# Slot-attention and FFN on one core: the weight products and the read-out of a unit made during the next unit

## The chip, the cores and the metric

One core of a Trainium2 chip runs the whole program. Its engines are TensorE (PE in the profile; its weight loads are PEld), VectorE (DVE), ScalarE (ACT), GpSimd (POOL) and SyncE (SP, which here issues most DMAs). The metric is the time of one execution on the device in microseconds, lower is better. A kernel's time is the median of its runs; beside it stands one profiled execution, whose trace gives the durations used below.

## The reference

Four sequences of 512 tokens (D = 512) go through LayerNorm, a slot attention with 16 heads, a residual, LayerNorm again, and a gated FFN whose weights are rounded to fp8 values (but computed in fp32), and a second residual. For each head, with 64 slots (M), keys of 64 and values of 128:

```python
z = jax.lax.cumlogsumexp(s, axis=2)
g = jnp.exp(jnp.concatenate([z[:, :, :1], z[:, :, :-1]], axis=2) - z)
p = jnp.exp(s - z)
# step over tokens
hk = hk * g_t[:, :, None, :] + k_t[..., None] * p_t[:, :, None, :]
ok = jnp.einsum('bhk,bhkm->bhm', q_t, hk)
pv = softmax(ok)
hv = hv * g_t[..., None] + p_t[..., None] * v_t[:, :, None, :]
ov = jnp.einsum('bhm,bhmv->bhv', pv_t, hv)
# then
o = o * rsqrt(mean(o * o) + EPS) * g_norm_weight
o = o * (gate * sigmoid(gate))
x = x + o.reshape(b, t, VALUE_DIM) @ Wo
x = x + ffn(layernorm(x))
```

## The kernel before

The kernel takes the recurrence apart into blocks of 64 tokens: products within a block under a triangular mask, and sums of states from block to block. A unit is a pair of heads (g, 0 to 7) of one sequence (b, 0 to 3). There are 32 units in the order b = 0, 1 for each g, then b = 2, 3 for each g. `first_unit` makes the first; `attention` makes each of the others, and within it carries out what is left of the unit in front (`before`). The FFN of the four sequences follows. The instructions of every engine stand in the order in which the code issues them, so each engine is a queue.

Precise products of wide matrices (128x512 results) are made of three products of parts rounded to fp32r: projections s, k, q, g (L517), v (L554) and o (L876), 12 matmuls for a projection and 6 for each of the four o blocks. Small products are plain fp32: transposes (L569, four for each tile: e, kn, oT, okn, w), and products of 64 rows: a = q and k within a block (L590), b = slot weights within a block (L590), sk and sv, the key and value states (L611), ok, the slot scores (L717 from states, L723 from a), and ov, the read-out (L803 from states, L813 from b).

The order of a unit before, as TensorE sees it: s, k, q, then the transposes e and kn; in an even unit v in four parts; between these the transposes oT of the unit in front; a, sk, sv; the two halves of g; ok; six matmuls of the front unit's o; okn; ten of o; w; four of o; b; four of o; ov. So b and ov belong to the unit itself. The work on other engines:

- `read_within` (L807) squares ov on ScalarE (L823) and sums it on VectorE (L824, L825), and GpSimd raises the sum to the power -1/2 (L828). `scale_output` (L833, VectorE, first head) and `scale_other` (L839, ScalarE in four pieces, second head) scale ov by it into og. They stand in the next unit, behind its s and k. `turn_output` (transposes oT, L855), `high_output` (L861) and `split_output` (L865, L866) make og times the gate into the three parts that o is made from.
- `softmax` (L738, L740), `softmax_exp` (L745), `slot_weights` (transposes w, then wT on VectorE, L784) and `move_weights` (L777, ScalarE, two copies) make the slot weights.
- `add_up` (L620) adds the states up: a copy (L622), a sum (L623) and, along the blocks, two more sums (L625). GpSimd then shifts states between halves of the partitions (L689 to L691 for keys, L768 to L771 for values).
- `project_output` (L870) copies each finished o block on ScalarE to y (L887), and GpSimd issues its accumulating DMA to the stream in HBM (L888).
- `fill`, `next_step`, `other`, `piece` take single pieces of side work from a list: splitting the next weights (L260, L266, L267; first half), LayerNorm of later sequences (L340 to L374), and rounding the FFN's weights (`quantize`, L451; second half).

PSUM has eight banks: four in a ring (`bank`, for transposes and most small products), two "proj" buffers (`ps3`, for projections and o blocks, taken in turn) and two "acc" buffers (`ps2`: a, ok and ov before; the FFN's sums later):

```python
            if name[0] == "a":
                p = ps2.tile([P, T], F32, tag="acc", name=f"ps_{name}_{h}")
            else:
                if turn[0] in held:
                    turn[0] = (turn[0] + 1) % BANKS
                p = bank(f"ps_{name}_{h}")
```

A buffer can be written again when its last reader is done. The token block that LayerNorm reads is loaded whole (four blocks of 128 tokens in one DMA, `load_tokens`, L308) and kept for the FFN's residual.

## Time and profile before

| what | value |
|---|---|
| median of 3 runs | 1402.9 us (1402.51 to 1403.57) |
| the profiled execution's own time | 1400.63 us |
| its span, first to last instruction | 1398.7 us |
| granted TensorE clock | 1.0 throughout |
| TensorE matmul, weight load busy | 1376.8, 1106.1 us |
| VectorE, ScalarE, GpSimd busy | 906.1, 701.4, 358.3 us |
| first FFN matmul, from the span's start | 1119.72 us |
| an odd unit, an even unit (second half, from s to s) | 28.58, 39.33 us |

A group's line gives start or line, engine, operation, output and inputs with shapes, count and duration; in square brackets stands how long the engine was idle in front of it and which instruction ended that. Matmuls overlap in TensorE's pipeline, so what one costs is read from start to start, not from its duration.

### The profile page before, as it was taken

To read this page: it belongs to the slowest core of one execution; us is meant where nothing else is said; L and a number is where in the kernel's file an instruction comes from. 1 tells how busy PE (TensorE), PEld (TensorE's weight loads), DVE (VectorE), ACT (ScalarE), POOL (GpSimd) and SP (SyncE) were. 2 spreads that over 40 slices of the span, in tenths; PEclk is the share of its full clock that TensorE was granted. 3 is DMA by queue.
4 is the path that set the end of the run, shared out by engine and by line. 5 is a ranking of instruction groups with operands and counts; after the bars stand their busy time and mean duration, and the time that the engine had idled before them with its cause. 6 is when DMAs were issued, how large, how long until landed. Compare 5 with 4: busy or idle time off the path is not lost.

```text
span 1398.7 us, 31065 instructions
## 1 busy us (share of the span) xinstructions
PE 1376.8 (98%) x13163; PEld 1106.1 (79%) x13163; DVE 906.1 (65%) x1625; ACT 701.4 (50%) x1327; POOL 358.3 (26%) x433
## 2 busy tenths in 40 slices
PE   8899999999999999999999999999999999999998
PEld 4678888888888877788888888887888788888886
DVE  6677656765676578756876677767776653535343
ACT  4557556655665566455544555455445633222221
POOL 2233323322333243223322332234124310000000
PEclk9999999999999999999999999999999999999999
DMA  8266646575556655456646574657455641101000
GB/s 323 105 195 228 198 113 174 190 248 148 149 184 216 179 176 154 119 167 197 185 133 189 189 216 110 189 189 232 116 174 172 217 117 16 61 0 60 1 31 30
DMA packets 80889, 213.03 MB, mean 152 GB/s; under 512 B 6168, under 2 KB 35120, under 8 KB 75568
## 3 DMA queue, kind: packets, MB, share of 16 engines
q1 hardware_dynamic: 62224, 177.49, 34.3%
q0 software_dynamic: 18528, 33.58, 15.8%
q8 instruction: 103, 1.69, 0.5%
q14 instruction: 34, 0.28, 0.1%
HBM read 107.23 MB, written 108.00 MB: 154 GB/s over the span
## 4 chain that ended last, share of the span: by engine, by line
PE 91%; DVE 5%; ACT 2%; DMA 1%; issue 1%; POOL 0%; SPq 0%; ACTq 0%; POOLq 0%; DVEq 0%
PE ps_o L876 14%; PE ps_g L517 11%; PE ps_v L554 10%; PE ps_s L517 6%; PE ps_fg L1099 6%; PE ps_fu L1099 6%; PE ps_k L517 6%; PE ps_q L517 5%; PE ps_fd L1160 3%; PE ps_fe L1160 3%; PE ps_ov L803 2%; PE ps_ov L813 2%; PE ps_sv L611 2%; PE ps_oT L569 2%; PE ps_b L590 1%; PE ps_w L569 1%
## 5 line engine op out<-in xcount | busy, mean ns | idle before, releaser
L876 PE MATMUL ps_o<-w_o,oT 128*128 128x512 f32 x768 | 212.0, 410 | 1.9 <-ACT w_o L260 1.2
L517 PE MATMUL ps_g<-xs,w_g 128*128 128x512 f32 x744 | 179.1, 396 | 0.0
L554 PE MATMUL ps_v<-w_v,xs 128*128 128x512 f32 x720 | 171.5, 393 | 0.0
L517 PEld LDWEIGHTS ps_g<-xs,w_g 128*128 128x128 f32 x744 | 137.1, 188 | 33.4 <-issue 5.3
L888 POOL DMA_DIRECT2D stream<-y x128 | 112.6, 940 | 192.7 <-ACT y L887 184.8
L876 PEld LDWEIGHTS ps_o<-w_o,oT 128*128 128x128 f32 x768 | 134.1, 188 | 30.9 <-ACT y L887 2.1
L554 PEld LDWEIGHTS ps_v<-w_v,xs 128*128 128x128 f32 x720 | 132.9, 188 | 26.2
L689 POOL COPY moved<-sk 64x192 f32<-64x192 f32 x32 | 10.9, 340 | 449.9 <-DVE sk L625 449.9
L1120 DVE SCALAR_TENSOR_TENSOR h<-ps_fu,scol,act 128x512 f32<-128x512 f32 x48 | 36.0, 750 | 114.5 <-PE ps_fu L1099 114.5
L1099 PE MATMUL ps_fg<-xs,wf 128*128 128x512 f32 x384 | 95.6, 391 | 0.0
L887 ACT COPY y<-ps_o 128x512 f32<-128x512 f32 x128 | 74.4, 581 | 40.9 <-PE ps_o L876 39.7
L1099 PE MATMUL ps_fu<-xs,wf 128*128 128x512 f32 x384 | 94.8, 389 | 0.0
L517 PE MATMUL ps_s<-xs,w_s 128*128 128x512 f32 x372 | 93.4, 400 | 0.0
L517 PE MATMUL ps_q<-xs,w_q 128*128 128x512 f32 x372 | 90.0, 391 | 2.1 <-DVE eT L642 2.1
L517 PE MATMUL ps_k<-xs,w_k 128*128 128x512 f32 x372 | 89.4, 389 | 0.0
L1099 PEld LDWEIGHTS ps_fu<-xs,wf 128*128 128x128 f32 x384 | 72.1, 188 | 15.0
L1099 PEld LDWEIGHTS ps_fg<-xs,wf 128*128 128x128 f32 x384 | 71.6, 188 | 14.8 <-issue 0.2
L517 PEld LDWEIGHTS ps_q<-xs,w_q 128*128 128x128 f32 x372 | 69.6, 188 | 17.0 <-DVE eT L642 2.5
L517 PEld LDWEIGHTS ps_s<-xs,w_s 128*128 128x128 f32 x372 | 67.4, 188 | 17.9 <-issue 3.4
L561 ACT COPY v<-ps_v 128x512 f32<-128x512 f32 x60 | 35.1, 585 | 92.8 <-PE ps_v L554 92.8
L517 PEld LDWEIGHTS ps_k<-xs,w_k 128*128 128x128 f32 x372 | 69.8, 188 | 14.5
L1126 ACT CAST both<-h 128x512 fp32r<-128x512 f32 x48 | 29.8, 620 | 96.7 <-DVE h L1120 96.7
(167 smaller groups left out, 2795.7 us busy)
## 6 DMA issues: line engine op xcount, KB each, us to landing
stream<-y POOLq DMA_DIRECT2D x128, 256.0 KB, 7.0
split_v<-w_v SPq DMA_DIRECT2D x4, 3072.0 KB, 11.5
split_g<-w_g SPq DMA_DIRECT2D x8, 1536.0 KB, 8.1
split_o<-w_o SPq DMA_DIRECT2D x8, 1536.0 KB, 7.1
w_v<-split_v SPq DMA_DIRECT2D x4, 3072.0 KB, 16.0
w_g<-split_g SPq DMA_DIRECT2D x8, 1536.0 KB, 7.3
w_o<-split_o SPq DMA_DIRECT2D x8, 1536.0 KB, 8.8
rounded<-qw SPq DMA_DIRECT2D x36, 256.0 KB, 2.2
```

What stands on the lines that cost most here:

```text
L517: nc.tensor.matmul(p, wt[self.nm][:, j, at : at + P], xs[self.b][i][:, c, :], start=(i == 0 and c == 0), stop=(i == 2 and c == KC - 1),)
L554: nc.tensor.matmul(p, xs[b][i][:, c, n * P : (n + 1) * P], wt["v"][:, j, c * 2 * HV : (c + 1) * 2 * HV], start=(i == 0 and c == 0), stop=( ...
L561: nc.scalar.copy(to, p)
L569: nc.tensor.transpose(pt[:, n, :], s, by)
L611: nc.tensor.matmul(pts[sub][half(h), n, :], left[half(sub), n, h * M : (h + 1) * M], right[half(sub), n, right0 + h * width : right0 + (h ...
L876: nc.tensor.matmul(self.p, self.oT[:, i, h, n * P : (n + 1) * P], wt["o"][:, j, h * D : (h + 1) * D], start=(i == 0 and h == 0), stop=(i = ...
L887: nc.scalar.copy(y, self.p)
L888: nc.gpsimd.dma_start(stream[self.b][n * P : (n + 1) * P, :], y, accum_op=ALU.add)
L1099: nc.tensor.matmul(pp, w[:, c * P : (c + 1) * P], xs[b][k][:, c, :], start=(c == 0 and k == 0), stop=(c == KC - 1 and k == 1),)
L1120: nc.vector.scalar_tensor_tensor(h, pu, us, act, ALU.mult, ALU.mult)
L1126: nc.scalar.copy(hi, h)
L1160: nc.tensor.matmul(sums[n], parts[k][:, n * P : (n + 1) * P], fw[c][2], start=(c == 0 and k == 0), stop=(c == NFC - 1 and k == 1),)
```

## The change

In every unit from the second on, b, the read-out ov and all that follows it are made for the unit in front, in one stretch with the unit's own a, key states and value states. `scale_output` and `scale_other` stand behind that stretch, with the load of ScalarE's silu table ahead of `scale_other`. The gate's second half follows, then ok, then oT of the unit in front, its parts, and the sums of the value states along the blocks (`add_along`); then the gate's first half, the softmax, and o in runs of 16 and 8. b takes the "acc" buffers and a the ring's banks; ov and ok stay in "acc". The last unit's b and ov are made at the head of the FFN. Tiles that now live longer have tags or second buffers of their own (eT, sg1, moved_v, moved_w, wT, the masked b). In o, the first two matmuls of the second block stand ahead of the last two of the first block. The two halves of a head pair are split side by side (`split_output`). LayerNorm's tokens are loaded in four single blocks into LayerNorm's own two tiles, the third and fourth as tiles come free, and normalised in place; the FFN loads its residual anew (`load_rest`), for the first sequence too. LayerNorm's measuring of the third and fourth block moves behind their loads. The FFN weights are rounded from three buffers instead of four, with four rounds in an even unit, two in the units of g = 1 and one in other odd units.

```diff
-    def load_tokens(b, source, pool=one, tag="tokens"):
-        x1[b] = pool.tile([P, NT, D], F32, tag=tag, name=f"x1_{b}")
-        nc.sync.dma_start(x1[b], source[b].rearrange("(n p) d -> p n d", p=P))
+    blocks_in = {}
+    def load_block(b, n, source):
+        blocks_in[b, n] = two.tile([P, D], F32, tag="xn", name=f"tokens_{b}_{n}")
+        nc.sync.dma_start(blocks_in[b, n], source[b][n * P : (n + 1) * P, :])
+    def load_tokens(b, source):
+        for n in range(2):
+            load_block(b, n, source)
+    def load_rest(b, places):
+        x1[b] = []
+        if len(places) == 1:
+            pool, tag = places[0]
+            x = pool.tile([P, NT, D], F32, tag=tag, name=f"x1_{b}")
+            nc.sync.dma_start(x, stream[b].rearrange("(n p) d -> p n d", p=P))
+            x1[b] = [x[:, n, :] for n in range(NT)]
+            return
+        for n, (pool, tag) in enumerate(places):
+            x = pool.tile([P, D], F32, tag=tag, name=f"x1_{b}_{n}")
+            nc.sync.dma_start(x, stream[b][n * P : (n + 1) * P, :])
+            x1[b].append(x)
...
-            if name[0] == "a":
+            if name[0] == "b":
...
-            a = one.tile([P, NT, SB], F32, tag=f"a{h}", name=f"{name}_{h}")
+            a = one.tile([P, NT, SB], F32, tag=f"{name[0]}{h}", name=f"{name}_{h}")
...
-    def add_up(own, pts, state):
+    def add_pairs(own, pts, state):
         nc.scalar.copy(own, pts[0])
         nc.vector.tensor_tensor(state, pts[1][:, : NT - 1, :], own[:, : NT - 1, :], ALU.add)
+    def add_along(state):
         for n in range(1, NT - 1):
             nc.vector.tensor_tensor(state[:, n, :], state[:, n, :], state[:, n - 1, :], ALU.add)
...
             self.left = [(n, i, j, h) for n in range(NT) for i, j in PAIRS for h in range(HG)]
+            self.left[4:8] = self.left[6:8] + self.left[4:6]
+            self.p = {}
...
-            self.z = one.tile([P, T], F32, tag="th", name=f"z_{self.u}")
+            self.z = one.tile([P, T], F32, tag="ok", name=f"z_{self.u}")
...
         def move_states(self):
             svo = self.svo
-            self.moved_v = moved = one.tile([P, NT, DV], F32, tag="kT", name=f"moved_v_{self.u}")
+            add_along(self.sv)
+            self.moved_v = moved = one.tile([P, NT, DV], F32, tag="moved_v", name=f"moved_v_{self.u}")
...
-            self.wT = one.tile([P, T], F32, tag="kn", name=f"wT_{self.u}")
+            self.wT = one.tile([P, T], F32, tag="wT", name=f"wT_{self.u}")
...
-            self.sg.append(one.tile([P, T], F32, tag=f"sg{h}", name=f"sg_{self.u}_{h}"))
+            self.sg[h] = (one, two)[h].tile([P, T], F32, tag=f"sg{h}", name=f"sg_{self.u}_{h}")
...
-        def split_output(self, h):
-            hi, lo, less = (self.oT[:, i, h, :] for i in range(3))
-            nc.vector.tensor_tensor(lo, self.sg[h], hi.bitcast(F32), ALU.subtract)
-            nc.vector.scalar_tensor_tensor(
-                less, lo.bitcast(F32), -1.0 / DELTA, hi.bitcast(F32), ALU.mult, ALU.add
-            )
+        def split_output(self):
+            parts = [[self.oT[:, i, h, :] for i in range(3)] for h in range(HG)]
+            for h, (hi, lo, _) in enumerate(parts):
+                nc.vector.tensor_tensor(lo, self.sg[h], hi.bitcast(F32), ALU.subtract)
+            for hi, lo, less in parts:
+                nc.vector.scalar_tensor_tensor(
+                    less, lo.bitcast(F32), -1.0 / DELTA, hi.bitcast(F32), ALU.mult, ALU.add
...
+    def silu():
+        nc.scalar.preload_act_table_set("silu_and_others")
...
         X.slots()
         load("s")
-        before.scale_output()
         need("k")
         X.keys()
         load("k")
         if not even:
             turning(True)
-        before.scale_other()
         X.running_sum()
         fill(more)
         need("q")
         X.queries()
         load("q")
-        if not even:
-            turning(True)
         X.turn_e()
+        X.turn_k()
+        X.inverse()
+        X.move_queries()
         if even:
-            X.turn_k()
-            X.inverse()
-            next_step()
             need("v")
-            X.values(0)
-            fill(more)
-            X.values(1)
-            before.turn_output(0)
-            before.high_output(0)
-            before.turn_output(1)
-            before.high_output(1)
-            fill(more)
-            X.values(2)
-            before.split_output(0)
-            next_step()
-            fill(more)
-            X.values(3)
-            before.split_output(1)
-            next_step()
-            fill(more)
-        else:
-            X.inverse()
-            before.turn_output(0)
-            X.turn_k()
-            before.turn_output(1)
-            before.high_output(0)
-            before.high_output(1)
+            for n in range(NT):
+                X.values(n)
+                next_step()
+                fill(more)
+        elif b > 1:
+            fill(1)
         if units[1] == (g, b):
             need(f"xs_{b - 1}")
+        while turned():
+            other(1)
+        before.weight_slot()
         X.query_key()
         X.key_states()
+        before.read_states()
+        before.read_within()
         X.value_states()
-        X.move_queries()
-        if not even:
-            before.split_output(0)
-            before.split_output(1)
-            fill(1)
+        before.scale_output()
+        silu()
+        before.scale_other()
         need("g")
+        X.gate(1)
+        X.gate_silu(1)
+        X.slot_scores()
+        before.turn_output(0)
+        before.high_output(0)
+        before.turn_output(1)
+        before.high_output(1)
+        before.split_output()
+        X.move_states()
         X.gate(0)
         X.gate_silu(0)
-        if even or b > 1:
-            next_step()
-        X.gate(1)
-        X.gate_silu(1)
         exp_and_log()
         load("g")
         if even:
...
         ahead()
         gated()
         need("o")
-        X.slot_scores()
-        before.project_output(6)
-        X.move_states()
         X.softmax()
+        before.project_output(8)
         X.softmax_exp()
-        fill(1)
-        before.project_output(10)
+        before.project_output(8)
         X.slot_weights()
         X.move_weights()
+        fill(1)
         next_step()
-        before.project_output(4)
-        X.weight_slot()
-        before.project_output(4)
+        before.project_output(8)
         load("o")
         X.softmax_sum()
-        if even or b > 1:
-            fill(1)
-        X.read_states()
         fill(1)
-        if even:
-            next_step()
-            if turned():
-                other(1)
-        X.read_within()
-        if not even and b < 2:
-            next_step()
-            if turned():
-                other(1)
+        next_step()
+        fill(1)
         return X
...
+                if (b, c) == (0, 0):
+                    before.weight_slot()
                 h = ffn_hidden(b, c)
                 if b == 0 and c == 0:
+                    before.read_states()
+                    before.read_within()
                     before.scale_output()
+                    before.left.sort()
                     before.scale_other()
                 if b == 0 and 0 < c < 3:
                     before.turn_output(c - 1, 2)
                     before.high_output(c - 1)
-                    before.split_output(c - 1)
+                    if c == 2:
+                        before.split_output()
                 if b == 0 and 2 < c < 3 + NT:
                     before.project_output(6)
+                if c == 1 and b == 0:
+                    load_rest(0, FFN_TOKENS[0])
                 if c == 1 and b + 1 < B:
-                    load_tokens(b + 1, stream, *((two, "v"), (one, "tokens"), (one, "y"))[b])
+                    load_rest(b + 1, FFN_TOKENS[b + 1])
```

## Prediction

> **What bounds the kernel now.** I read the page's busy times and chain first, then the timeline of one unit in the second half (786 to 815 us), all engines, then the waits of TensorE.
>
> ```profile
> PE 1376.8 (98%) x13163; PEld 1106.1 (79%) x13163; DVE 906.1 (65%) x1625; ACT 701.4 (50%) x1327; POOL 358.3 (26%) x433
> PE 91%; DVE 5%; ACT 2%; DMA 1%; issue 1%; POOL 0%; SPq 0%; ACTq 0%; POOLq 0%; DVEq 0%
> ```
>
> TensorE (PE) is busy 98% of the span and is 91% of the chain; its waits add up to some 17 us, with none over 3.0 us. So a part of the change is worth only what it takes from, or puts into, the stream of matmuls. That stream has a price of its own for changing between wide matmuls (128x512) and small ones (64-row products, transposes):
>
> ```profile
> 809.69 0.66 PE L569 MATMUL ps_w<-idents,ok 128*128 128x128 f32 x4
> 810.10 1.18 PE L876 MATMUL ps_o<-w_o,oT 128*128 128x512 f32 x4
> 811.20 0.69 PE L590 MATMUL ps_b<-wT,eT 64*64 64x64 f32 x32
> 811.83 1.20 PE L876 MATMUL ps_o<-w_o,oT 128*128 128x512 f32 x4
> 812.95 0.32 PE L803 MATMUL ps_ov<-moved_v,moved_w 64*64 64x128 f32 x1
> ```
>
> Read start to start. Undisturbed, 12 matmuls of ps_k took 2.72 us (789.12 to 791.84), 0.227 each, so four should take 0.91; here four ps_o between small groups took 1.10 and 1.12, and ps_b took 0.63 where ps_a, with the same shapes but small neighbours, took 0.51.
>
> **The change, by stretches of one odd unit (28.58 us from s to s: 786.27 to 814.85).** All starts below are of that unit, or of the next where ps_w and ps_o are meant.
>
> *Taken out: changes of kind.* b and ov leave the place between ps_o's and join kn, a, sk and sv in one small stretch. From the end of w to the end of s the old order took 1.10 + 0.63 + 1.12 + 1.90 (ov) + 2.85 (s) = 7.60. The same work costs 1.91 (eight ps_o behind w) + 0.515 (b priced as a) + 1.79 (ov without its 0.11 us exit) + 2.72 (s as k) = 6.93. The rest of the unit (oT behind ok, g in two halves, o in 16 + 8) gains another 0.11 by the same counting: 0.78 in all. In an even unit sk and sv no longer interleave (0.18 back): about 0.6. The 31 units behind the first are 16 odd and 15 even: 16 x 0.78 + 15 x 0.62 = **-21.8 us**.
>
> *Added: a wait at ps_ok.* ps_b, ps_ov and ps_ok now share the two "acc" buffers, in this order, within one unit. Until now s, k and q (8.3 us) lay between the read-out ov and ps_ok's group; now it is sv and half of g. ps_ok may not start before ov's results have been read by scale_output (VectorE) and scale_other (ScalarE), and these wait for a chain over three engines:
>
> ```profile
> 786.27 3.01 PE L517 MATMUL ps_s<-xs,w_s 128*128 128x512 f32 x12
> 786.37 1.09 ACT L823 ACTIVATE og<-ps_ov 128x512 f32<-128x512 f32 x2 [0.77 <-PE ps_ov L813]
> 787.00 1.28 DVE L824 TENSOR_REDUCE rs<-og 128x4 f32<-128x512 f32 x2 [2.28 <-ACT og L823]
> 788.32 0.17 DVE L825 SCALAR_TENSOR_TENSOR rs<-rs,sq 128x8 f32<-128x8 f32 x1
> 788.64 1.67 POOL L828 TENSOR_TENSOR rs<-rs,mhalf 128x8 f32<-128x8 f32 x1 [2.42 <-DVE rs L825]
> 790.34 0.69 DVE L833 TENSOR_TENSOR og<-ps_ov,rs 128x512 f32<-128x512 f32 x1 [0.32 <-POOL rs L828]
> 792.58 1.15 ACT L839 ACTIVATE og<-ps_ov,rs 128x128 f32<-128x128 f32 x4
> 797.49 1.13 PE L611 MATMUL ps_sv<-v,e 64*64 64x128 f32 x28
> 798.56 5.76 PE L517 MATMUL ps_g<-xs,w_g 128*128 128x512 f32 x24
> ```
>
> Squares, two sums, rs, GpSimd's power, then the scaling: the power ends at 790.31. L839 came late only because it was queued behind kT; freed of that it runs 790.35 to 791.50. TensorE left ov at 786.27, or 786.17 without the exit. So ps_ok can go 5.38 us after ov (791.50 + 0.05 - 786.17). What lies between now: sv 1.07 (797.49 to 798.56) and half of g (5.68 / 2, plus 0.10 for the change of kind) 2.94: 4.01. TensorE stands 1.37 us in each of 31 units: **+42 us**. The ACT table load that moves ahead of scale_other (1.28 us) and the svo copy (0.59) end 1.1 us before the power does, so they cost nothing; without that cover they would lengthen the wait by what is left of them. Over the 32 units the quickest power ended 0.1 sooner and the slowest 0.3 later than here: 1.25 to 1.65 per unit, 39 to 51 in all.
>
> *Added: a wait at the next unit's ps_s.* With b and ov gone, only eight ps_o (1.91) lie between w and s. ps_s takes the buffer of the third ps_o, whose copy to y stands on ScalarE behind the two copies of moved_w, and these wait for wT:
>
> ```profile
> 810.38 0.69 DVE L784 TENSOR_TENSOR wT<-ps_w,rzT 128x512 f32<-128x512 f32 x1 [0.33 <-PE ps_w L569]
> 811.10 0.82 ACT L777 COPY moved_w<-wT 64x256 f32<-64x256 f32 x2 [1.00 <-DVE wT L784]
> 811.95 0.59 ACT L887 COPY y<-ps_o 128x512 f32<-128x512 f32 x1
> ```
>
> From w's start (809.69) that copy ends at 812.54, 2.85 later; s is wanted 0.41 + 1.91 = 2.32 after w: 0.56 of standing with the 0.03 handoff. In ten units of the first half a weight split (L260, 622 ns) is queued ahead of that copy: 1.18. In four units with LayerNorm transposes around the eight ps_o it is about 0.3. 10 x 1.18 + 17 x 0.56 + 4 x 0.3 = **+22.5 us**. Ends: 12, if the split comes later in the queue and the copy earlier; 30, if every unit pays some 0.97.
>
> *The softmax.* VectorE's queue from ps_ok to w: okT 0.75, two sg 1.40, lo 1.37, less 1.38, two sv sums, mx 0.69, ok 0.69, then ScalarE's exp 0.63. The sv sums (L625) move here from behind ps_sv:
>
> ```profile
> L625 DVE TENSOR_TENSOR sv<-sv x64: 291/705/874, 44.2 to 1105.2; 128x128 f32<-128x128 f32 x64
> ```
>
> 291 with GpSimd at rest (two cases), 705 beside its additions. In the new place GpSimd has nothing to do until they are done: 0.58 for two. With 0.2 ahead of okT and 0.15 of handoffs the chain is 7.85; TensorE's cover is oT 0.8 + g 2.85 + okn 0.36 + sixteen ps_o 3.9 = 7.9. It just fits: **0**. At the row's mean (555 each, 1.11) it would be late by some 0.47 in 31 units, +15: the upper end. The lower end is -4, the 0.12 by which w already waits for exp today.
> The Trainium skill (GPSIMD Engine Reference, Specifications) says that GpSimd shares its SBUF interfaces with VectorE and collides with instructions of two SBUF inputs. By it the sums cost their undisturbed 291, so nothing here; by the mean of the row it would be +15.
>
> *Small terms.* In odd units kn's copy ends just when sk wants it, so sk waits for the handoff: 16 x 0.05 = 0.8. In the eight odd units of the second half the last quantize step (two of 0.69) stands ahead of b's masks on VectorE, which then start 2.25 us after q instead of 1.6; the second is 0.4 late for ov, which needs its buffer: 3.2. In the FFN the first oT has 3.9 us of cover (16 matmuls and a change of kind) for scale_output, which needs 4.9: 1.0. Sum **+5**. Lifted: 0.67 at ps_ok in three even units (706.93 to 746.94 is 40.01 against 39.33), and two stops at oT for a bank held by LayerNorm (1.26 and 1.45): **-4.7**, at worst +3 if the block loads take their place. The token loads by block (four of 256 KB for one of 1 MB, per LayerNorm, and four more for the first FFN block) go through SP's queue; the weight loads behind them are issued a unit ahead (28 us; the slowest, w_v, lands in 16.0), which hides a block's wait for its tile. If that cover went, a late weight would stop a projection for as long as the load is late. GpSimd's powers stand ahead of its moved_v work and behind moved, which ends 0.3 before the power is due: nothing.
>
> Sum: -21.8 + 42 + 22.5 + 0 + 5 - 4.7 = +43. The profiled execution took 1400.6, of which 1398.7 is the span; its sum is 1443.6. The median of the runs lies 2.3 above that execution: **1446 us**.
>
> **Rivals.** *The softmax chain binds as well* (20%): VectorE late at w by 0.47 in every unit, 1446 + 15 = 1461. For it: a margin of 0.05 in 7.9. Against: the two undisturbed sums.
> *The wait at ps_s is mostly hidden* (11%): if something else delays TensorE between w and s, or the copy slips ahead; 1446 - 22 = 1424. Against: ScalarE's queue is in program order.
> *ps_ok does not wait* (7%; the case that ends on the other side). Place: the first matmuls of ps_ok; price: the whole 42 us; it decides if the chain from ov to scale_other takes 4.0 us instead of 5.4. Then -21.8 + 22.5 + 5 - 4.7 = +1, 1404: no change; with half of the wait at ps_s gone too, 1393. Against: in none of the 32 units did the power end sooner than 4.0 us after ov, and scale_other's 1.15 comes behind it.
> *The change doesn't do what it says*: b and ov do stand beside a, sk and sv in the order of the built program, in all 31 units; no chance is kept for it.
>
> **How the numbers follow.** Forecast 62%, 1446, its own range 1432 to 1458. The softmax rival takes the range up to 1466; the ends of ps_s's wait and of the switches take it down to 1424. Below lie the case without the ps_ok wait and half of the tail. A measurement here can tell 0.2% (2.8 us) from no change: faster 4%, same 3%, slower 93%.
>
> **What would show it.** In the new profile: ps_o in runs of 16 and 8 with fewer slow first matmuls; TensorE idle some 1.3 us ahead of ps_ok, released by VectorE's og or ScalarE's og; idle some 0.5 ahead of ps_s, released by ScalarE's y; w waiting no longer than today; sv sums near 291. An odd unit of 29.9 us. The prediction is wrong if TensorE arrives at ps_ok and finds it free, or if w's wait grows past 0.5.

## The result, and the profile after

After the change the kernel takes 1524.4 us (median of four runs, 1517.3 to 1528.1) against 1402.7 before (1400.8 to 1403.6): a ratio of 1.086, 95% interval 1.082 to 1.090. It is slower, as forecast, but by 122 us where 43 were forecast, and outside the range. The profiled execution took 1528.06 us, its span 1526.4.

The page of after first: busy times, granted clock in 40 slices, and the chain by engine.

```profile
PE 1394.3 (91%) x13163; PEld 1130.3 (74%) x13163; DVE 874.7 (57%) x1625; ACT 700.8 (46%) x1327; POOL 336.0 (22%) x433
PEclk9899999999999999799999999999999999999999
PE 67%; DVE 11%; DMA 9%; ACT 6%; POOL 4%; issue 3%; SPq 0%; POOLq 0%; DVEq 0%; ACTq 0%
```

The matmuls are the same 13163. TensorE was busy 98% of the span and 91% of the chain; now it is busy 91% and holds 67% of the chain. Two shares are new in kind: DMA has 9% where it had 1%, "issue" 3% where it had 1%. The prediction's only term for DMA is the +3 that the block loads could cost at worst. The list of TensorE's waits shows where they fall (tile and line that waited, what it waited for; us in total, times, longest):

```profile
PE ps_ok L750 <- DVE og L867: 25.7, 27, 1.2
PE ps_ov L837 <- DVE b L623: 19.1, 6, 5.5
PE ps_s L544 <- ACT y L923: 16.1, 27, 0.9
PE ps_xn L380 <- DVE tokens L371: 14.1, 5, 8.0
PE ps_a L617 <- ACT qT L685: 9.4, 6, 2.8
PE ps_ov L847 <- issue: 5.1, 2, 2.7
PE ps_s L544 <- DMA w_s<-split_s: 5.1, 1, 5.1
...
PE ps_e L596 <- ACT eT L675: 4.6, 3, 2.0
PE ps_q L544 <- DVE eT L674: 4.4, 3, 1.6
PE ps_o L912 <- DVE w_o L267: 4.1, 2, 3.6
```

Two kinds stand here side by side. Rows one and three have 27 entries, all short: they come in nearly every unit, and they are the two waits that the prediction names. The other rows have one to six entries of up to 8.0 us: stops of some units only, which the prediction does not have. No row has ps_w: the softmax rival did not come.

Cut the span at the first matmul of each ps_s and it falls into units (us; steady: what an undisturbed unit of the second half has more than before, 1.15 in an odd unit (29.71 to 29.72 against 28.55 to 28.57) and 1.06 in an even one (40.39 against 39.33)):

| stretch | before | after | more | steady part |
|---|---|---|---|---|
| head, unit 0 | 52.8 | 62.6 | 9.8 | 0 |
| unit 1 | 45.1 | 46.9 | 1.8 | 1 |
| units 2 to 13 | 408.4 | 457.4 | 49.0 | 13 |
| units 14, 15 | 62.6 | 76.9 | 14.2 | 2 |
| unit 16 | 41.6 | 50.6 | 9.0 | 1 |
| units 17 to 30 | 478.0 | 509.2 | 31.3 | 13 |
| unit 31 | 31.3 | 40.4 | 9.2 | 1 |
| FFN | 279.0 | 282.4 | 3.5 | 0 |

So the steady cost, 16 x 1.15 + 15 x 1.06, is about 34 us (some 2 less, since three even units were 0.67 longer before). The forecast was 43. The column "more" sums to 128, the difference of the two profiled spans (the medians differ by 122). The other 94 are in places, and these must be explained one by one. The windows of three units of after (window, us; then busy us and count of PE, PEld, DVE, ACT, POOL; granted clock, DMA share, GB/s) show the two kinds:

```profile
1060.66:1090.37 29.71, 28.25 (x349) 23.33 (x349) 18.63 (x36) 16.78 (x34) 9.70 (x12) 1.00 0.78 253
598.20:643.70 45.50, 33.02 (x358) 26.26 (x357) 26.34 (x52) 20.76 (x42) 12.58 (x17) 0.87 0.32 77
643.70:694.30 50.60, 44.18 (x413) 35.55 (x413) 26.13 (x52) 20.39 (x38) 9.85 (x13) 0.95 0.38 120
```

In the undisturbed odd unit TensorE stands 1.46 us at the full clock. Units 15 and 16 stand 12.5 and 6.4 us, at a granted clock of 0.87 and 0.95: there a stop also makes the matmuls behind it slower. This price can be read by itself; in such stretches the granted clock is 0.50 (after, columns as above):

```profile
642.32:649.14 6.82, 5.43 (x13) 4.30 (x14) 1.39 (x3) 0.00 (x0) 0.70 (x1) 0.50 1.05 352
1007.54:1014.37 6.83, 3.97 (x73) 4.00 (x77) 2.80 (x9) 0.29 (x1) 1.79 (x3) 0.50 0.29 83
```

After has twelve of them, 61.4 us together; before has none from 5 us to 1397 us.

### The profile page after: what moved, and what is told of

Its sections match the earlier page's. It is cut to its first block, busy times and chain, and to the rows that moved or that the text cites. A ratio compares the mean times of both kernels' runs of the same rounds, so it can differ in the third digit from the quotient of the medians.

```text
span 1526.4 us, 31065 instructions
## 1 busy us (share of the span) xinstructions
PE 1394.3 (91%) x13163; PEld 1130.3 (74%) x13163; DVE 874.7 (57%) x1625; ACT 700.8 (46%) x1327; POOL 336.0 (22%) x433
## 4 chain that ended last, share of the span: by engine, by line
PE 67%; DVE 11%; DMA 9%; ACT 6%; POOL 4%; issue 3%; SPq 0%; POOLq 0%; DVEq 0%; ACTq 0%
PE ps_o L912 9%; PE ps_v L581 7%; PE ps_g L544 6%; PE ps_fg L1108 6%; PE ps_fu L1108 6%; PE ps_s L544 4%; PE ps_k L544 4%; POOL rs L862 3%; PE ps_q L544 3%; PE ps_fd L1169 3%; PE ps_fe L1169 3%; PE ps_ov L837 2%; DVE rs L858 2%; PE ps_oT L596 2%; DMA rounded<-qw 2%
## 5 line engine op out<-in xcount | busy, mean ns | idle before, releaser
L912 PE MATMUL ps_o<-w_o,oT 128*128 128x512 f32 x768 | 198.2, 406 | 6.3 <-DVE w_o L267 4.1
L544 PE MATMUL ps_g<-xs,w_g 128*128 128x512 f32 x744 | 189.2, 403 | 2.3 <-issue 2.3
L912 PEld LDWEIGHTS ps_o<-w_o,oT 128*128 128x128 f32 x768 | 139.2, 191 | 39.6 <-ACT y L923 6.1
L544 PE MATMUL ps_s<-xs,w_s 128*128 128x512 f32 x372 | 97.3, 412 | 24.8 <-ACT y L923 16.1
L544 PEld LDWEIGHTS ps_q<-xs,w_q 128*128 128x128 f32 x372 | 69.6, 188 | 19.9 <-issue 5.6
```

Of the source, the lines that this page charges most:

```text
L544: nc.tensor.matmul(p, wt[self.nm][:, j, at : at + P], xs[self.b][i][:, c, :], start=(i == 0 and c == 0), stop=(i == 2 and c == KC - 1),)
L912: nc.tensor.matmul(self.p[n], self.oT[:, i, h, n * P : (n + 1) * P], wt["o"][:, j, h * D : (h + 1) * D], start=(i == 0 and h == 0), stop=( ...
```

## The experiments

All runs beside runs of the kernel before on the same chip. "Against after" is by medians.

| run | median us | ratio to before, 95% | against after |
|---|---|---|---|
| ok_in_ring | 1493.7 | 1.065 [1.061, 1.068] | -30.7 |
| y_before_moved | 1528.1 | 1.090 [1.088, 1.092] | +3.7 |
| spread_splits | 1527.7 | 1.089 [1.085, 1.094] | +3.3 |
| rounding_as_before | 1514.2 | 1.080 [1.079, 1.082] | -10.2 |
| two_more_places | 1508.7 | 1.075 [1.073, 1.077] | -15.7 |
| blocks_in_time | 1511.7 | 1.078 [1.076, 1.080] | -12.7 |
| all_five | 1449.5 | 1.033 [1.032, 1.035] | -74.9 |
| nothing_late | 1432.6 | 1.022 [1.021, 1.023] | -91.8 |
| splits_like_before | 1428.2 | 1.018 [1.016, 1.020] | -96.2 |
| last_blocks | 1417.2 | 1.011 [1.010, 1.013] | -107.2 |
| b_at_head | 1410.8 | 1.007 [1.005, 1.009] | -113.6 |
| pieces_after_w | 1420.2 | 1.012 [1.010, 1.013] | -104.2 |

### The two waits of every unit

**ok_in_ring.** ps_ok takes two banks of the ring, so it no longer needs the buffers that ov holds.

```diff
-            pok = [
-                ps2.tile([P, T], F32, tag="acc", name=f"ps_ok_{self.u}_{sub}") for sub in range(2)
-            ]
+            pok = [bank(f"ps_ok_{self.u}_{sub}") for sub in range(2)]
```

> The changed kernel with ok's two results in banks of the ring instead of the two acc buffers; nothing else. Theory A: ok waits only because it takes the buffers that ov's scaling still reads (25.7 us over 27 units in the trace of the changed kernel). In the ring it need not; the next reader of the scaled og is oT, 1.37 us of ok later, and the chain of 5.38 us behind ov then has 4.01 + 1.37 us of cover, so at most 0.1 us a unit is left: 20 to 26 us less, about 1500. Rival B: the wait only moves, to oT or to the softmax chain: no more than 7 us less, 1517 or above.

Measured: 30.7 us less. The wait is gone from the list, and an undisturbed odd unit is 28.36 long instead of 29.71 to 29.72 (window of this run, columns as above):

```profile
1029.92:1058.28 28.36, 27.95 (x349) 23.07 (x349) 18.62 (x36) 16.74 (x34) 9.69 (x12) 1.00 0.82 267
```

That is more than the 20 to 26 of theory A. So the wait costs 1.36 in an odd unit (1.37 was forecast) and 1.32 to 1.35 in an even one. The row above shows only 0.95 for one (25.7 / 27): the rest is in starts that the wait delays without counting as idle time. Over 31 units 1.36 would be 42; it was 30.7 by the medians and 37.7 by the two profiled spans. What is missing lies in units with other stops: 23 and 26, for instance, have a stop of 2.2 and 2.6 us called "issue" in this run. The mechanism and its price stand; it is not what the prediction missed.

**y_before_moved.** The third o block's copy to y comes ahead of moved_w on ScalarE:

```diff
         X.slot_weights()
-        X.move_weights()
         fill(1)
         next_step()
         before.project_output(8)
+        X.move_weights()
```

> The changed kernel with the two moved_w copies issued behind the last two y copies instead of ahead of them. Theory A: ps_s waits (16.1 us over 27) because the y copy of the third o block queues behind them on ScalarE: 13 to 16 us less, about 1509. Rival B: ps_s waits for the copy's own length and the matmul before it; what is ahead of it in the queue doesn't matter: within 4 us of the changed kernel.

Measured: no gain; the median is 3.7 higher, within the scatter of the two kernels' runs. By its number that is rival B. Its cause is not rival B's, though: where nothing else is late, a window of an odd unit of the second half is 0.72 shorter than after's:

```profile
1057.41:1086.41 29.00, 27.96 (x350) 23.40 (x348) 18.62 (x36) 16.94 (x33) 9.65 (x13) 1.00 0.80 254
```

The trace has the wait's cause as forecast, too: on ScalarE the copies to y stand behind the two of moved_w, which waited 1.44 for wT (last bracket: idle before, and what ended it; this is after's timeline).

```profile
1059.13 0.83 ACT L811 COPY moved_w<-wT 64x256 f32<-64x256 f32 x2 [1.44 <-DVE wT L818]
1059.98 1.08 ACT L923 COPY y<-ps_o 128x512 f32<-128x512 f32 x2
```

In the first half the saved 0.72 went into the next stop: ps_q's wait for eT rose from 4.4 to 19.9 us. A small wait just in front of a larger one is worth nothing alone.

### The first half: where the pieces of the weight splits stand

In the first half each weight is loaded into one of two raw buffers and split by pieces (L260 on ScalarE, then VectorE). Before the change such pieces (placed by `fill`) began on VectorE at 0, 6.4, 17.8, 22.6 and 27.1 us from s in unit 3. In the new order they begin at 1.7, 3.0, 6.9, then 32.9 and 34.8 (the unit is stretched). When three pieces come at once the two raw buffers are empty, and the next load cannot have landed. ScalarE's queue is in order; in unit 3 of after:

```profile
148.22 0.64 ACT L698 ACTIVATE rzT<-rzT 128x512 f32<-128x512 f32 x1
152.15 0.63 ACT L260 ACTIVATE w_s<-raw_s 128x512 fp32r<-128x512 f32 x1 [3.29 <-DMA raw_s<-in_L_attn_Ws_dram]
152.69 0.58 ACT L685 ACTIVATE qT<-ps_q 128x512 f32<-128x512 f32 x1
```

ScalarE stands 3.29 us for a load that SP issued at 148.90, when the piece begun at 6.9 us had freed the raw buffer. qT is ready to be made but queued behind, and `ps_a <- qT` (9.4 us in the waits) is the price. eT pays in the same way (4.6 and 4.4).

**spread_splits** moves one of three late places behind scale_other and one behind softmax_exp, in units 1 to 13:

```diff
         before.scale_other()
+        spread = 0 < units.index((g, b)) < len(units) // 2 - 2
+        if spread:
+            fill(1)
...
         X.softmax_exp()
+        if spread:
+            fill(1)
...
-        fill(1)
+        if not spread:
+            fill(1)
```

> The changed kernel, with two of the three pieces of side work that stand at the end of a unit (units 1 to 13) moved into its middle: one behind the scaling of og, one behind the softmax's exp. Theory A: the first half's units lose time (about 31 us of their 49 us of excess is not the two predicted waits) because the pieces of weight splitting are bunched, three at the end of a unit and up to five at the start of the next, and the two raw buffers run dry: ScalarE stands at the split's first copy for a DMA, with eT or qT queued behind it. Spread, the loads are in time and TensorE's clock stays up: 18 to 30 us less, 1495 to 1506. Rival B: the raw loads are late because the queue that issues them stands in front of other transfers; the pieces' places matter little: less than 8 us.

Measured: no gain, a miss, and by its number rival B. Units 2 to 13 fell by 7.3 in the profiled execution, but unit 14 rose by 6.3: TensorE waits 2.3 and 4.5 us there at ps_xn for LayerNorm's tokens, against 1.4 once in after. Why the tokens are late there stays open.

**two_more_places** adds the two places and keeps the late ones, in units 2 to 13:

```diff
         before.scale_other()
+        spread = 1 < units.index((g, b)) < len(units) // 2 - 2
+        if spread:
+            fill(1)
...
         X.softmax_exp()
+        if spread:
+            fill(1)
```

> The changed kernel with two more places for a piece of weight splitting in units 2 to 13 (behind the scaling of og, behind the softmax's exp), and the three at the unit's end kept. The run that moved two pieces instead of adding places left units 2 to 13 at 450.1 us (457.4 in the changed kernel, 408.4 before), and there one piece more was still undone at the end of a unit. Theory A: the first half stalls because the pieces come late: w_o's pair is put ahead of w_v's last, the raw buffers stay taken, and the loads of the next s, k and q are issued only when their splits are due; with two more places they are done ahead: units 2 to 13 at 425 to 435 us, the whole 20 to 32 us less. Rival B: pieces in the middle of a unit delay okT or wT by as much as they save: units 2 to 13 above 448.

Measured: 15.7 us less; units 2 to 13 take 440.6 instead of 457.4. That lies between the two theories (425 to 435, above 448). So the places do set a loss there: of the 36 us beyond the steady part they brought back 17.

### Blocks and weights that come late

**blocks_in_time.** Sequence 1's last two blocks are loaded at once into spare buffers; sequence 3's first loads are issued later; the FFN's first two late blocks come a unit earlier; w_o's last pieces are made behind scale_other.

```diff
     def load_tokens(b, source):
         for n in range(2):
             load_block(b, n, source)
+        if b == 1:
+            for n, tag in ((2, "eT"), (3, "sg1")):
+                blocks_in[b, n] = two.tile([P, D], F32, tag=tag, name=f"tokens_{b}_{n}")
+                nc.sync.dma_start(blocks_in[b, n], source[b][n * P : (n + 1) * P, :])
...
         before.scale_other()
+        need("o")
...
                     need("xs_2")
+                    load_tokens(3, x)
                     transposing[0] = layernorm(3, 1, source=x)
...
+            if (g, b) == (NG - 1, 2):
+                pair = one.tile([P, 2, D], F32, tag="raw0", name="tokens_pair")
+                for n in (2, 3):
+                    blocks_in[0, n] = pair[:, n - 2, :]
+                    nc.sync.dma_start(pair[:, n - 2, :], stream[0][n * P : (n + 1) * P, :])
...
-            if (g, b) == (NG - 1, 1):
-                load_tokens(3, x)
```

> The changed kernel with its token blocks loaded in time: the third and fourth block of sequence 1 at once into the idle second buffers of eT and sg1, those of the FFN's first sequence at the start of unit 30 into the rounding's raw0, the loads of sequence 3 issued in the middle of unit 15 instead of ahead of it, and the last pieces of w_o done behind the scaling of og. Theory A: the block loads are what lengthens units 0, 16 and 31 (8.7, 9.0 and 9.2 us over before): in 0 and 31 VectorE stands at a load that was issued only when a transpose freed a buffer, in 16 TensorE waits for w_s, whose reload stands in SyncE's queue behind a load that waits 40 us for a buffer; and w_o's pieces, forced late, are what lengthens 15 (12.3 us). Unit 0 at about 37, 15 at 36 to 38, 16 at 44 to 46, 31 at 33 to 36, the whole 20 to 28 us less. Rival B: the four units are long because VectorE's queue is full there, whenever the loads land: less than 10 us in all.

Measured: 12.7 us less, between theory A (20 to 28) and rival B (below 10). Unit 15 fell from 45.5 to 39.1 and unit 31 from 40.4 to 33.1; units 0 and 16 stayed (44.2 and 50.7). Two readings of it. First, unit 16: SP's queue in after stands at a block load, with the next weights queued behind it.

```profile
598.45 40.52 SPq L312 DMA_DIRECT2D tokens<-_attn_hidden_states_dram  x3
639.01 0.42 SPq L247 DMA_DIRECT2D w_s<-split_s  x1
```

The blocks of sequence 3 wait 40.52 us for their buffers, and w_s can only then be issued: TensorE waited 5.1 us for it. With the load moved SP is free (blocks_in_time):

```profile
591.35 2.60 SPq L312 DMA_DIRECT2D tokens<-_attn_hidden_states_dram  x2
596.40 0.33 SPq L247 DMA_DIRECT2D w_s<-split_s  x1
```

and the wait for w_s is gone, but unit 16 is as long: now the block itself is late (VectorE waits 4.25 for it), and ps_s waits 5.3 for xs. The load is needed early and must not stand in front of the weights; only a buffer that is free early gives both. Second, unit 31 in after, on VectorE:

```profile
1207.98 1.22 DVE L696 TENSOR_TENSOR_SCAN z<-eT 128x512 f32<-128x512 f32 x1 [0.70 <-ACT eT L675]
1214.76 0.69 DVE L362 BATCH_NORM_STATS2 stats<-tokens 128x6 f32<-128x512 f32 x1 [5.56 <-DMA tokens<-stream]
...
1219.40 0.74 DVE L623 TENSOR_TENSOR b<-ps_b,tri 128x256 f32<-128x256 f32 x2
```

VectorE stands 5.56 us for a token block, in front of b's mask; ps_ov waits 5.5 for b. Nothing of this unit needs the block. It is the queue that does the harm.

**rounding_as_before.** The changed kernel gave four sets of FFN weights to round to an even unit of b = 3, with three load buffers; here they are dealt as before:

```diff
-                for _ in range(min(0 if units[i] == (0, 2) else 4 if g % 2 == 0 else 2 if g == 1 else 1, to_come[0])):
+                for _ in range(min(0 if units[i] == (0, 2) else 2 if g % 2 else 4 if b == 2 else 3, to_come[0])):
```

> The changed kernel with the rounding of the FFN's weights dealt to the units as before the change (odd 2 sets, even 4 for b = 2 and 3 for b = 3; the change has 4 in every even unit, 1 in most odd ones). Theory A: the units of b = 3 with 4 sets stall (21, 25 and 29 lose 4.4, 8.1 and 3.5 us against before) because VectorE waits for the fourth set's load ahead of b's masks: 8 to 14 us less, about 1513. Rival B: three load buffers instead of four are too few for any dealing: the waits move to the odd units, less than 4 us.

Measured: 10.2 us less, within theory A. In unit 25 of after VectorE waits 3.96 and 4.77 us for weights to round, again ahead of b's masks:

```profile
1001.11 0.43 DVE L488 TENSOR_SCALAR q<-qw 128x512 int32<-128x512 int32 x1 [3.96 <-DMA qw<-in_L_ffn_gate_w_dram]
...
1009.15 0.43 DVE L488 TENSOR_SCALAR q<-qw 128x512 int32<-128x512 int32 x1 [4.77 <-DMA qw<-in_L_ffn_up_w_dram]
1009.83 0.75 DVE L623 TENSOR_TENSOR b<-ps_b,tri 128x256 f32<-128x256 f32 x2
```

Units 21, 25 and 29 came to 40.41, 41.42 and 40.41, near the undisturbed 40.39.

### All together, and what was left

**all_five**: ok_in_ring, y_before_moved, rounding_as_before, two_more_places and blocks_in_time in one kernel, with no other edit.

> All edits together: ok in the ring, y copies ahead of the moved_w copies, two more places for the splits, rounding dealt as before, blocks and w_o in time. Theory A: what the changed kernel lost is these five things, each on top of the others: 31 + 20 (0.7 a unit, as the second half's undisturbed units show, once the first half is not held by late pieces) + 10 + 25 + 24 off 1524, so 1405 to 1425; an odd unit of the second half at 27.7, an even one at 38.4. Rival B: something else holds it, and the removed waits come back elsewhere: above 1440.

Measured: 74.9 us less, where the five alone sum to 65.6; in the undisturbed units the y edit is worth its 0.72 on top of ok's 1.36. Still, 1449.5 lies above 1440, where rival B begins: something else holds the kernel too. TensorE now waits 12.6 us for qT (9.4 in after), once for 7.5. An undisturbed odd unit now shows no idle TensorE at all, and is shorter than before's 28.55:

```profile
996.64:1024.29 27.65, 27.65 (x350) 23.15 (x348) 21.80 (x43) 16.95 (x33) 9.81 (x13) 1.00 0.94 285
```

So the new order without the two waits gains 0.92 in an odd unit (from 28.57) and 1.02 in an even one (39.33 to 38.31). The prediction gave this term, 0.78 and 0.6, to changes of kind; no run splits it further.

**nothing_late** adds to all_five: sequence 1's four blocks are measured at once, sequence 3's are loaded early into a free raw buffer, w_o's last two pieces are pulled out alone in unit 15, the first split copy of the next weight is no longer let through behind the running sum, and in unit 0 the gate's silu goes ahead of the slot weights.

```diff
-        fill(more)
+        fill(more, True)
...
-        ahead_of = NT if source is None else 2
+        ahead_of = NT if source is None or b == 1 else 2
...
+        if b == 3:
+            pair = one.tile([P, 2, D], F32, tag="raw1", name="tokens_pair_3")
+            for n in range(2):
+                place(b, n, source, pair[:, n, :])
+            return
...
+        if late:
+            pull("o")
         before.scale_output()
...
         X.gate(1)
-        X.slot_weights()
-        X.move_weights()
-        next_step()
         X.gate_silu(0)
         X.gate_silu(1)
         exp_and_log()
+        X.slot_weights()
+        X.move_weights()
+        next_step()
```

> The run of all edits (1449.5), with what its trace shows late put right: the first split copy of the next matrix no longer issued on ScalarE ahead of qT in a place in front of it (it stood up to 7.5 us there for a load); all four blocks of sequence 1 measured at once, so that GpSimd's power for them isn't queued behind the state moves (6.7 us in unit 0); the blocks of sequence 3 loaded before they are measured, two of them into an idle raw buffer; w_o's two last pieces of unit 15 alone around the scaling of og, without LayerNorm's items ahead of them; the first unit's silu ahead of its slot weights (3.6 us). Theory A: with these gone only the order of a unit is left, and that is faster than before: an undisturbed odd unit is 27.65 us against 28.57, an even one 38.31 against 39.33 to 40.0 in the run of all edits. Unit 0 near 36, units 2 to 13 at 396 to 412 us (429.1; before 408.4), 15 at 33 to 36 (41.1), 16 at 41 to 44 (49.0); the whole 1392 to 1415. Rival B: the first half has too little room for the splits in this order, and the wait turns up at another load: units 2 to 13 above 422, the whole above 1425.

Measured: 16.9 us less than all_five, but by both of its signs this is rival B: units 2 to 13 took 428.2 (above 422), the whole 1432.6 (above 1425). Unit 0 fell from 44.7 to 35.2, its time before the change (35.7). blocks_in_time had left it at 44.2: with the load there in time, the wait at ps_xn only fell from 8.0 to 6.8. The rest is order. In after, VectorE normalises sequence 1's fourth block ahead of its third, and the fourth's power stands on GpSimd behind the move of the states:

```profile
49.05 0.99 POOL L805 TENSOR_TENSOR svo<-svo,sv 64x384 f32<-64x384 f32 x1
50.11 0.55 POOL L365 TENSOR_TENSOR rstd<-rstd,mhalf 128x1 f32<-128x1 f32 x1
```

So the third block, whose own power had ended at 44.63, is normalised only behind that, and ps_xn starts at 51.84. In nothing_late, where all four blocks are measured first, the powers stand in front of the move:

```profile
34.79 0.55 POOL L386 TENSOR_TENSOR rstd<-rstd,mhalf 128x1 f32<-128x1 f32 x1 [0.46 <-DVE rstd L385]
36.30 0.34 POOL L743 COPY moved<-sk 64x192 f32<-64x192 f32 x1 [0.96 <-DVE sk L677]
```

The wait at ps_xn is 1.4 there. The earlier silu has a share in the gain as well: s, which waited 3.6 us for it, now waits 1.8 (for xs). Unit 16 only fell to 48.1 (44.3 in the next run, 41.6 before the change).

**splits_like_before** makes one late piece in odd units and two in even ones from unit 2 on, and puts measures of late blocks ahead of normalising.

```diff
-        fill(1)
+        if late:
+            fill(1)
+        if not spread:
+            fill(1)
...
-        fill(1)
+        if not spread or even:
+            fill(1)
```

> The last run (1432.6) with its places for side work set so that the pieces of the splits come in the order that the kernel before had: one piece at a unit's end instead of three (two in units with v) from unit 2 on, so that w_o's pair no longer stands ahead of w_v's last and ahead of eT; and the measuring of the late token blocks of sequences 2 and 3 and of the FFN's first put in front of their normalising, so that GpSimd's answer isn't waited for block by block. Theory A: the odd units of the first half (32 to 33.5 us, against 27.65 for an undisturbed one) lose their 4 to 5 us to the pieces bunched between two units and to the loads behind them; now units 2 to 13 at 395 to 408 us (428.2; before 408.4), 15 and 16 together 3 to 8 us less (85.3), the whole 1392 to 1410. Rival B: the places don't decide; what holds the first half is the transfers themselves (the split parts written out share the queues with the raw loads): units 2 to 13 stay above 420.

Measured: 4.4 us less by the medians, none by the profiled executions, where opposite parts cancel. Units 2 to 13 fell by 7.7, to 420.6; units 16 and 31 fell by 3.8 and 3.6; the head with units 0 and 1 rose by 3.7, and units 17 to 30 by 11.4. By its sign (above 420) this is just rival B, but its cause is not in the trace: in units 2 to 13 ScalarE's waits for loads have fallen to 10.0 us (43.1 in after, 11.3 before), and of the 14.2 us for which TensorE waits there 9.7 are stops called "issue" (last section). The rise in units 17 to 30 is a late block once more, one that this edit put there: VectorE measured the pair of the FFN's blocks in unit 30 before it had landed.

```profile
1091.97 0.69 DVE L384 BATCH_NORM_STATS2 stats<-tokens_pair 128x6 f32<-128x512 f32 x1 [8.39 <-DMA tokens_pair<-stream]
```

**last_blocks** measures that pair behind unit 30's softmax_exp instead:

```diff
         X.softmax_exp()
...
+        if (g, b) == (NG - 1, 2):
+            late_measures[0]()
+            other(2)
...
-                late_measures[0]()
```

> The last run (1428.2), with the FFN's last two blocks of sequence 0 measured behind unit 30's softmax instead of at its start, where VectorE stood for their loads with b's masks behind them (unit 30: 38.1 us, 28.2 in the two runs before it). Theory: unit 30 near 28.5, the clock there not lowered, 31 at 29 to 31, the whole 9 to 11 us less, 1417 to 1420. Otherwise a wait shows up in unit 31 and the whole stays above 1424.

Measured: 11.0 us less, as expected, of which 10.0 in units 17 to 30. So the same measuring, ahead of or behind the landing, is worth 10 us.

**b_at_head** takes b (`weight_slot`) out of the dense stretch of small products and puts it ahead of s:

```diff
+        if units.index((g, b)) > 1:
+            before.weight_slot()
...
-        before.weight_slot()
+        if units.index((g, b)) == 1:
+            before.weight_slot()
```

> The same, with b's 32 products at the head of the unit, ahead of s, instead of ahead of a (from unit 2 on). The run of small products a, sk, ov, sv is then 148 long instead of 180. Theory A: the stops of 2.3 to 3.6 us that no releaser explains, all within this run of small products and all while a block of the program's own instructions lands, come of TensorE taking these short instructions faster than they are delivered; with a shorter run they become fewer (17 us of them in the last run, at most 9 here), and b's masks are no longer what ov waits for. Against it stands one more switch between kinds of products, 0.2 to 0.4 us a unit, 6 to 12 us in all: 1408 to 1422. Rival B: the stops don't come of the run's length: as many of them, and the switch on top, 1424 to 1432.

Measured: 6.4 us less, 1410.8, the best of all and within theory A. An undisturbed odd unit is 0.44 longer than all_five's (28.09; one more change of kind), but TensorE's stops called "issue" fell from 15.8 to 6.1 us, and its time at half clock from 27.3 to 6.8 us (see the last section).

**pieces_after_w** moves the piece at softmax_exp behind slot_weights, and lets VectorE copy e in odd units of the first half, with scheduled work let through ahead of scale_output:

```diff
-            nc.scalar.copy(self.e, pt)
+            if self.g % 2 and self.b < 2:
+                nc.vector.tensor_copy(self.e, pt)
+            else:
+                nc.scalar.copy(self.e, pt)
...
+        if 1 < units.index((g, b)) < len(units) // 2 - 2:
+            ahead()
...
         X.softmax_exp()
-        if spread:
-            fill(1)
...
-        if not spread:
-            fill(1)
+        fill(1, spread)
```

> The last run (1410.8), in which an odd unit of the first half still takes 29.5 to 30.5 us against 28.09 in the second, and units 2 to 13 take 415.6 (before 408.4). Three edits in units 2 to 13: the split piece behind the softmax's exp goes behind wT (there it delayed wT by 0.7 us); the first split copy of the piece that stands behind the scaling of og is issued ahead of the silu table's load, while ScalarE waits for GpSimd anyway (it delayed okT by about 1 us); and in odd units VectorE instead of ScalarE copies e, so that kn's copy, which the key states wait for, comes 0.6 us sooner. Theory A: each of these lies on the path: 1 to 1.8 us for each of the nine units that splits lengthen, units 2 to 13 at 400 to 408 us, the whole 1398 to 1405, no different from before. Rival B: what lengthens them is TensorE's instructions coming late or the loads; units 2 to 13 above 412.

Measured: 9.4 us more than b_at_head, a miss. The loss is spread over nearly all stretches of the profiled execution (+2.1 at the head and in unit 0, +3.0 in units 2 to 13, +2.6 in unit 15, +4.0 in units 17 to 30), also where the three edits do nothing: in units 23 and 26 it is a stop called "issue". In units 2 to 13 two effects stand against each other. The six odd units are 4.1 us shorter together; units 4, 8 and 12 are 7.8 longer. There ScalarE stands 6.5 to 7.2 us for a raw load with eT behind it, against 2.7 to 3.3 in b_at_head:

```profile
170.25 0.63 ACT L267 ACTIVATE w_g<-raw_g 128x512 fp32r<-128x512 f32 x1 [6.51 <-DMA raw_g<-in_L_attn_Wg_dram]
170.79 0.61 ACT L709 ACTIVATE eT<-eT 128x512 f32<-128x512 f32 x1
```

Which of the three edits makes that load late is not told apart, as they were not run one by one.

## Why the prediction was right and wrong

*The direction, and the wait at ps_ok: right.* 1.37 was forecast for an odd unit, 1.36 measured (1.32 to 1.35 in an even one). It is the largest steady cost, and without it the kernel was still 6.5% slower. One reading behind it was too narrow: "the slowest 0.3 later than here" holds for the second half; in twelve units of the first half of before the power ended 0.6 to 2.0 us later than in the unit shown.

*The wait at ps_s: right mechanism, size a little off.* 0.56 forecast, 0.72 measured. The two sizes of the forecast, 1.18 in ten units of the first half and 0.56 in 17 others, are in the list too, lower, as idle time understates them: ten entries of 0.90 to 0.93 and 17 of 0.40 to 0.42.

*Changes of kind: right, too small.* 0.78 and 0.6 forecast, 0.92 and 1.02 measured with both waits gone. By this term alone the new order is worth some 30 us (16 x 0.92 + 15 x 1.02), not 21.8. With the two waits it gives 1.36 + 0.72 - 0.92 = 1.16 for an odd unit, where 1.15 was measured.

*The softmax: right.* No wait at ps_w. The sv sums kept their undisturbed time in the new place, 0.61 us for two (0.58 forecast):

```profile
1054.61 0.61 DVE L655 TENSOR_TENSOR sv<-sv 128x128 f32<-128x128 f32 x2
```

*Small terms.* sk does wait for kn, by up to 0.3 in some units (1.3 us in all; 0.8 forecast). The first oT in the FFN waits 0.9 (1.0 forecast); the FFN is 3.5 longer, as 1.9 us of ov now stand in it. An odd unit was forecast at 29.9 and took 29.7.

So the steady part came to about 32 to 34 against the forecast 43, and all its causes were those named. The step that failed is the one on everything that does not come in every unit: the prediction put it at -4.7 us, +3 at worst, and it came to some 94. The points below overlap, as a stop of points 1, 2, 3 and 5 also brings point 4 with it:

1. *Block loads.* The prediction said that the weight loads' lead of a unit "hides a block's wait for its tile", lifted 4.7 us and gave +3 as the worst case. It costed SP's queue by its usual lead, and did not follow one block load through the queue to see when its buffer comes free. Measured: 40.52 us of standing on SP ahead of unit 16's weights; 5.56 us on VectorE in unit 31; unit 0 delayed by 8.0 at ps_xn because measuring by block put LayerNorm's power on GpSimd behind the moves of states (the prediction weighed GpSimd's queue for the power of the read-out alone). The excess of units 0, 15, 16 and 31 is 39 us (8.7 + 12.3 + 9.0 + 9.2), of which some 4 steady.
2. *The order of side work.* The list of `fill` places was in the diff, and the prediction counted the L260 piece only where it delays y. Where the pieces stand against the raw buffers was not worked out. Of the 36 unsteady us in units 2 to 13 two more places brought back 17. With the late ones thinned and without the two steady waits (last_blocks) the units take 416.7, which is still 21 above twelve undisturbed ones (6 x 27.65 + 6 x 38.31 = 395.8). The mechanism did go: ScalarE waits 10.4 us for loads there (43.1 in after), and TensorE 3.8 for qT and eT (18.4). But TensorE's stops called "issue" rose from 2.2 to 9.4.
3. *The dealing of the rounding.* The prediction noted only that one step stands ahead of b's masks (3.2 us in the first case of that kind), not that four sets in a unit want more than three buffers: 10.2 us.
4. *A granted clock of 1.0 was assumed.* In after the clock fell to 0.5 in twelve stretches, 61.4 us together, and TensorE is busy in 48.9 of them. There matmuls of a projection or an o block follow one another at some 0.43 us instead of 0.227, and 28 matmuls of ov take 1.90 us (from 1012.19) where 27 take 0.94 (from 776.83). If all of it takes twice as long, the price is half of 48.9, some 24 us (an estimate). These stretches stand at or behind stops of the other points, for instance at 625.3 to 635.5 and 642.3 to 649.1 in units 15 and 16.
5. *"issue" stops*, 9.9 us in after (5.1, 2.5 and 2.3 in the list of waits), of which the list of before has none (see the last section).

Not all of the 94 is settled. With both steady waits gone, 30 us below before's span would be 1369; last_blocks' span is 1413.7. So some 45 us are still there. The list names 15.8 of them as "issue", and the half clock (27.3 us) takes some 14 by the same estimate.

Points 1 to 3 have one shape, and the runs show it three times: a DMA is late for work that no one needs soon (a piece of a later weight, a later sequence's block, an FFN weight); the engine that does it takes its queue in order; and behind it stands work that TensorE needs now (qT and eT, b's masks, w_s). In the order of before, ScalarE too waited 11.3 us for loads in units 2 to 13, but nowhere that made TensorE wait. The change moved the places and the loads without moving the two together.

No version beat the kernel before. b_at_head, the best, is 0.7% slower, although TensorE's own busy time is below before's 1376.8:

```profile
PE 1365.8 (97%) x13163; PEld 1105.7 (79%) x13163; DVE 888.0 (63%) x1625; ACT 703.5 (50%) x1327; POOL 340.1 (24%) x433
```

It gains 7.7 us in units 17 to 30 and 2.2 in unit 31, and loses 7.2 in units 2 to 13, 3.0 in the FFN and 6.1 in the head and units 0, 1 and 14 to 16. So the idea is sound where the side work is on time, and whether the first half could be brought there as well stays open.

## What to carry to other kernels

When an order of work is rewritten, price the stream that bounds the kernel and then every queue that carries side work beside it: for each DMA that an engine waits for, write down when its buffer comes free, when it lands, and what stands behind the waiting instruction in that engine's queue. A mean busy share, or "it is issued a unit ahead", is not that price. Add to each stop of TensorE the half clock that can follow it, some 24 us here by the estimate above. When several waits stand close together, take them all away before judging one alone: here an edit worth 0.72 us in an undisturbed unit measured as nothing by itself.

## What the hardware showed that was not expected

*Stops called "issue".* TensorE stood several times in the middle of a group for which nothing was missing, always in or soon behind the dense stretch of small products (b, a, sk, ov and sv: 180 matmuls in some 4 us). Before and behind such a stop in after (timeline of TensorE):

```profile
776.83 0.94 PE L847 MATMUL ps_ov<-v,b 64*64 64x128 f32 x27
...
780.48 0.32 PE L847 MATMUL ps_ov<-v,b 64*64 64x128 f32 x1 [2.71 <-issue]
```

and what the DMA engines moved from 777.9 to 779.2 (queue, kind: packets, MB, share of the 16 engines):

```profile
q1 hardware_dynamic: 97, 0.51, 96.1%
...
q8 instruction: 1, 0.02, 4.6%
```

One block of the instruction queue (16 KB, 778.08 to 779.03) lands within the stop. In after and last_blocks seven stops of this kind, of 2.2 to 3.4 us start to start, each have such a block landing within them or just at their start (893.85 to 896.55 with a block at 894.19 to 895.23; in last_blocks 841.25 to 843.82 with one at 841.45 to 842.42). That alone says little, since a block also lands within 17 of the 28 dense stretches of after that have no stop. What says more is when TensorE goes on: 1.45 us after the landing here (779.03 to 780.48), and 1.2 to 1.6 us after one in each of the 82 stops of TensorE called "issue" (0.3 us or longer) in the traces of all runs. With b taken out of the stretch, which leaves 148 matmuls, the sv entry of the waits fell from last_blocks

```profile
PE ps_sv L672 <- issue: 11.3, 5, 3.2
```

to b_at_head

```profile
PE ps_g L578 <- issue: 2.2, 2, 1.4
PE ps_sv L672 <- issue: 2.2, 2, 1.9
...
PE ps_ok L782 <- issue: 1.2, 2, 1.0
```

All such entries together fell from 15.8 to 6.1 us. So it is the landing of a block of instructions that ends these stops; the narrow 1.2 to 1.6 us shows it. That short matmuls use instructions up faster than they are delivered is argued: it fits the fall, but most such stretches have no stop, and what lets one stretch run dry and not the next stays open. A full DMA is not needed for it: over two of the stops the DMA engines' share was 1.00 (777.50 to 780.48) and 0.00 (274.54 to 276.74).

*The clock after stops.* In after each of the six stops of more than 3.5 us brought a stretch at half clock, and so did six of eleven between 1.9 and 3.1 us (one of 2.2 us more stands just ahead of a longer one). The shortest is the 1.93 us in front of 276.74; the one of 2.71 us shown here brought none, nor did before's two (2.10 and 2.95).

```profile
277.09:280.50 3.41, 3.41 (x15) 2.50 (x9) 1.16 (x2) 2.83 (x6) 1.24 (x1) 0.50 0.00 0
```

All twelve stretches last 3.41 us or two or three times that, and the clock's full stretches between them are whole multiples of 3.41 us too: the changes lie on a fixed grid, wherever the stop falls. The Trainium skill (TensorE: Matmul & The Clock Gate, Part 1: The HAM clock gate) has the clock set by how busy TensorE was in a free-running window of about 3.4 us; the grid agrees with that. Its table asks for an idle window of that length before the clock falls; here 1.93 us of idle time were enough once, and another time 3.03 us were not. That the place of the stop on the grid decides fits these rows, but is not tested by them.
